# Exchanging the engines of two products in a selective-scan kernel: VectorE multiplies by B, GpSimd by C, in one ring of nine tiles

## The chip, the cores and the metric

The kernel runs on one core of a Trainium2 chip. The metric is the device time of one execution in microseconds; the figure for a kernel is the median of its runs. Before the change that is 13688.56 us (three runs, 13686.65 to 13699.43).

Engine names in the profile: PE is TensorE (PEld its weight loads), DVE is VectorE, ACT is ScalarE, POOL is GpSimd, SP is SyncE, whose queue issues all DMAs of this kernel.

## The reference, cut to what matters

The program is four network layers in a row on a 4 x 64 x 64 x 128 input. Layers 0 and 1 hold selective scans over images of L = 4096 pixels; layers 2 and 3 (a gated neighbourhood layer and a window attention) are not touched. The scan, for every image, direction k (4), channel d and state n (16), is

```
dA = exp(delta_t[d] * A[d, n])
h  = dA * h + (delta_t[d] * u_t[d]) * B_t[n]
y_t[d] = sum over n of h[d, n] * C_t[n]
```

Layer 0 has 128 channels, layer 1 has 256; B and C depend on time and state, not on the channel. Softplus, normalisation, 3x3 convolutions and projections stand before and after.

## The kernel before, in words

**Tiling.** A *unit* is a group of 8 channels x 16 states, which fills 128 partitions, by TS = 1024 pixels in fp32. 16 units (NG) make a *step*: 128 channels, one direction, a quarter of the image. 16 steps make a *task* (NU = 256 units): one image and 128 channels. There are 4 tasks in layer 0 and 8 in layer 1, so 12 x 256 = 3072 units, 1536 pairs and 192 steps.

**What a unit does.** `load` (L436) has the SP queue fetch delta*u of the 8 channels from DRAM, each repeated over the 16 states, into a tile `dub`. `times_b` (L443) multiplies it on GpSimd by `repB`, B repeated over the channels in SBUF by a DMA (`repeat`, L371), and writes one half of a two-unit tile `h`. `decay` has TensorE spread delta over the states into a PSUM tile `da` (L451, two buffers) and ScalarE turn it into exp(delta*A) in place (L453). `scan` (L462) is VectorE's recurrence, in place on `h`. After each second unit VectorE multiplies the pair by C (L472), from `h` into another tile `hc`; C is a PSUM tile of one buffer that `bring_c` (L492) makes with TensorE once a step. `save` (L483) has ScalarE copy the last column of the states for the next step. `add_up` (L547) has TensorE sum `hc` over the states into a PSUM tile `yps`, which `sum_so_far` opens and `keep` (L557) copies out.

**The order.** No scheduler moves these instructions: `run` writes the order out by hand, one pass of its loop per unit u, and each engine takes its own instructions in that order. In pass u: scan(u); times_b(u+3); bring_c at the first unit of a step; save of the pair just ended; decay(u+2); add_up of the pair just ended; then pieces of the *preparation* of a later step (`prepare`: delta, delta*u and their DMAs `dud`, `dp`, `repB`), begun AHEAD = 22 units early, and pieces of *side work* (convolutions, projections and norms before and after the scans, helpers at L97); then load(u+6). A small model of each engine's backlog, `Plan`, decides how many pieces fit into a pass: `slot` enters what the pass itself costs TensorE, ScalarE and GpSimd, and a piece is taken if the engines would reach it soon enough. DMAs of a step are posted with due times in units (`post`). When all scans are done, a rest of layer 1 runs, then layers 2 and 3.

**Buffers.** `dub` has 5 tiles of one unit, `h` 3 tiles of two units, `hc` 2 tiles of two units, `da` 2 and `C` 1 (PSUM), `repB` and `dp` 2.

Of the kernel before, what the change touches and what calls it, by code (L numbers as in the profile page):

```python
# [9 lines left out]
F32 = mybir.dt.float32  # L10
# [7 lines left out]
P = 128  # L18
H = 64
# [5 lines left out]
NS = 16  # L25
ND = 4
NG = 16
TS = 1024
# [77 lines left out]
UNIT = 3.6  # L106
# [7 lines left out]
class Plan:  # L114
# [22 lines left out]
    def post(self, chain, issue, due=0.0):  # L137

        if self.running:
            self.posted.append((chain, max(self.done, due), issue))  # L140
        else:
            issue()
# [11 lines left out]
    def slot(self, u, sums, copies):  # L154
        at = self.at
        self.now = u * UNIT
        self.flush()
        at["PE"] = max(at["PE"], self.now) + 1.1
        at["ACT"] = max(at["ACT"], at["PE"]) + 1.1
        at["POOL"] = max(at["POOL"], self.now - 1.2) + 2.4  # L160
        at["PE"] += sums
        at["ACT"] += copies

# [56 lines left out]
class ScanWeights:  # L220


    def __init__(self, tc, C, pool, layer, d_xp, d_dtw, d_av):
        nc = tc.nc
        self.layer, self.nct, self.rank = layer, TILES[layer], RANKS[layer]
        nct, rank = self.nct, self.rank
        self.nc, self.pool, self.d_xp, self.d_dtw = nc, pool, d_xp, d_dtw
        n = ND * nct * NG
        av = pool.tile([P, n + 2 * ND * nct], F32, name=f"av{layer}")
        nc.sync.dma_start(out=av, in_=d_av)  # L230
        self.a = av[:, 0:n]
        nc.scalar.activation(self.a, self.a, AF.Exp)
        nc.vector.tensor_scalar_mul(self.a, self.a, -1.0)
        self.dtb = av[:, n : n + ND * nct].rearrange("p (k t) -> p k t", k=ND)
        ds = av[:, n + ND * nct :].rearrange("p (t k) -> p t k", t=nct)
        self.dsum = pool.tile([P, nct], F32, name=f"dsum{layer}")
        nc.vector.reduce_sum(self.dsum, ds, axis=AX.X)

        self.pick = pool.tile([P, P], F32, name=f"pick{layer}")
        one, two = (C.ident[:, i * H + rank + NS : i * H + rank + 2 * NS] for i in range(2))  # L240
        both = [P, NS, P // NS]
        nc.vector.tensor_add(
            self.pick.rearrange("p (n i) -> p n i", n=NS),
            one.unsqueeze(2).to_broadcast(both),
            two.unsqueeze(2).to_broadcast(both),
        )
# [24 lines left out]


NU = ND * NSTEP * NG
AHEAD = 22


class Scans:
# [47 lines left out]
    def prepare(self, t, step):  # L325

        nc, W, half, post = self.plan, t.W, self.half, self.plan.post
        begin = self.plan.now
        k, c = t.steps[step]
        R = W.rank  # L330
# [35 lines left out]
        out = t.prepared[step] = {"xd": xd}  # L366

        def repeat():
            out["B"] = self.tile("repB", 2)
            src = bass.AP(xdd.tensor, xdd.offset + R * TS, [[TS, NS], [0, 8], [1, TS]])  # L370
            nc.sync.dma_start(out=out["B"], in_=src)  # L371

        post("rep", repeat, max(begin + 5 * UNIT, ready))

        bias = W.dtb[:, k, t.ct : t.ct + 1]
        delta, low = self.tile("delta", 1), self.tile("low", 1)
        for i in range(HALVES):
# [5 lines left out]
                start=True,  # L383
# [25 lines left out]
        def own(part, j):  # L409
            if j == part == 0:  # L410
                out["delta"] = self.tile("dp", 2, shape=(96, 4, TS), dtype=BF16)
            nc.sync.dma_start(
                out=out["delta"][32 * part : 32 * part + 32, j, :], in_=parts[32 * j : 32 * j + 32, part, :]
            )

        for i in range(12):
            j, part = divmod(i, 3)
            post("rep", lambda part=part, j=j: own(part, j), begin + (9 + 0.7 * i) * UNIT)
        yield ""

    def unit(self, u):
# [7 lines left out]
    def load(self, u):  # L429
        t, step, jj, j, g = self.unit(u)  # L430
        if g == 0:
            self.plan.flush("prep")
        dud = t.prepared[step]["du"]
        dub = self.live["dub", u] = self.tile("dub", 5)
        src = bass.AP(dud.tensor, dud.offset + 8 * g * TS, [[0, NS], [TS, 8], [1, TS]])
        self.nc.sync.dma_start(out=dub, in_=src)  # L436

    def times_b(self, u):
        t, step, jj, j, g = self.unit(u)
        if u % 2 == 0:  # L440
            self.live["h", u // 2] = self.tile("h", 3, shape=(P, 2, TS))
        dbu = self.live["h", u // 2][:, u % 2, :]
        self.nc.gpsimd.tensor_mul(dbu, self.live.pop(("dub", u)), t.prepared[step]["B"])  # L443

    def decay(self, u):
        t, step, jj, j, g = self.unit(u)
# [8 lines left out]
    def scan(self, u):  # L455

        nc = self.nc
        t, step, jj, j, g = self.unit(u)
        way = slice(None, None, -1) if t.steps[step][0] >= 2 else slice(None)
        da, pair = self.live.pop(("da", u)), self.live["h", u // 2]  # L460
        h = pair[:, u % 2, :]
        nc.vector.tensor_tensor_scan(  # L462
            h[:, way],
            da[:, way],
            h[:, way],
            0.0 if step % NSTEP == 0 else t.states[step - 1][:, u % NG : u % NG + 1],
            ALU.mult,
            ALU.add,
        )
        if u % 2:  # L470
            hc = self.live["hc", u // 2] = self.tile("hc", 2, shape=(P, 2, TS))
            nc.vector.tensor_mul(hc, pair, t.prepared[step]["C"].unsqueeze(1).to_broadcast([P, 2, TS]))  # L472

    def save(self, p):

        t, step, jj, j, g = self.unit(2 * p)
        pair = self.live.pop(("h", p))
        i = 2 * p % NG
        if i == 0:
            t.states[step] = self.tile("state", 2, shape=(P, NG))  # L480
        if step % NSTEP < NSTEP - 1:
            end = 0 if t.steps[step][0] >= 2 else TS - 1
            self.nc.scalar.copy(t.states[step][:, i : i + 2], pair[:, :, end])  # L483

    def bring_c(self, u):

        t, step, jj, j, g = self.unit(u)
        c = t.prepared[step]["C"] = self.psum.tile([P, TS], F32, name="C", tag="C", bufs=1)
        rows = t.W.rank + 2 * NS
        for i in range(HALVES):  # L490
            at = slice(i * H, i * H + rows)
            self.nc.tensor.matmul(  # L492
                c[:, self.half(i)], t.W.pick[at, :], t.prepared[step]["xd"][at, :], start=True, stop=True
            )


# [36 lines left out]

    def add_up(self, p):

        hc = self.live.pop(("hc", p))
        for v in range(2):
            t, step, jj, j, g = self.unit(2 * p + v)
            for i in range(HALVES):
                at = i * H + 32 * v  # L540
                out = self.live["yps"][at : at + 32, :]
                if t.steps[step][0] % 2 == 0:
                    rhs = hc[:, v, self.half(i)]
                else:
                    rhs = hc[:, v, :].rearrange("p (r i l) -> p r i l", i=HALVES, l=ROWS)[:, :, i, :]
                    out = out.rearrange("p (r l) -> p r l", l=ROWS)
                self.nc.tensor.matmul(out, self.C.gather[jj], rhs, start=False, stop=jj == 3)  # L547
# [19 lines left out]
    def run(self, between):  # L567
# [7 lines left out]
            pass  # L575
        self.plan.start()
        pieces, fetch, fetched = Lane(self.plan, "prep", iter(())), iter(()), 0
        for u in range(-7, total):
            if u >= 0:
                self.scan(u)  # L580
            if 0 <= u + 3 < total:
                self.times_b(u + 3)
            if u >= 0 and u % NG == 0:
                self.bring_c(u)
            if u > 0 and u % 2 == 0:
                self.save(u // 2 - 1)
            if 0 <= u + 2 < total:
                self.decay(u + 2)
            if u > 0 and u % 2 == 0:
                self.add_up(u // 2 - 1)  # L590
            if u > 0 and u % 8 == 0:
                self.keep(u - 1)
            if u > 0 and u % 8 == 1:
                self.sum_so_far(u - 1)
            even, eighth, first_one = u % 2 == 0, u % 8 == 1, u % NG == 0
            self.plan.slot(
                u, 1.6 * even + 1.0 * eighth + 2.0 * first_one, 0.25 * even + 0.7 * (u % 8 == 0)
            )
            ahead, rest = divmod(u + AHEAD, NG)
            if rest == 0:  # L600
# [19 lines left out]
            if u >= 0:  # L620
# [1 line left out]
                if self.later:  # L622
                    self.later.pop(0)()
                between(n, i)
            if 0 <= u + 6 < total:
                self.load(u + 6)
        self.add_up(total // 2 - 1)
        self.save(total // 2 - 1)
        self.keep(total - 1)
        while self.later:  # L630
            self.later.pop(0)()

# [524 lines left out]
def scan_layers(tc, C, nb, x_in, d0, s0, d1, s1, out):  # L1157

    nc = tc.nc
    with ExitStack() as es:  # L1160
# [24 lines left out]
        def between(n, i):  # L1185
# [1 line left out]
            nonlocal lane, current, credit  # L1187
            u = n * NU + i

            done = group[n] - (1 if i >= 8 or n and group[n - 1] == group[n] else 2)  # L1190
            left, rate = -(lane.count if lane else 0), 0.0
            for name, b, after, before in ([current] if lane else []) + work:
                left += PIECES[name]
# [15 lines left out]
        with tc.manual_schedule():  # L1209
            for _ in side.pre0(0):  # L1210
# [8 lines left out]
                Aside(side, n, spans, bank)  # L1219
                for n, bank in enumerate(  # L1220
                    lambda name=name, bufs=bufs: psum.tile([P, TS], F32, name=name, tag=name, bufs=bufs)[:, 0:T]
                    for name, bufs in (("C", 1), ("da", 2))
                )
            ]
            lanes = [lane.post1(nb - 1, range(n, NCH, 3), wt) for n, lane in enumerate(lanes)]
# [959 lines left out]
```

## Time and profile before

| what | value |
|---|---|
| median of three runs | 13688.56 us |
| the profiled execution, own time | 13702.12 us |
| its span (first to last instruction) | 13699.8 us |
| first scan starts, last product with C ends | 204.7 us, 11445.5 us |
| VectorE, GpSimd busy over the span | 11766.7 us (86%), 9928.8 us (72%) |
| TensorE, ScalarE busy over the span | 10024.2 us (73%), 7913.4 us (58%) |
| mean granted TensorE clock | 0.737 of full |
| DMA: bytes, share of 16 engines' span | 2474.92 MB, 73.6% (the SP queue) |

How to read it: the profile records each instruction's engine, line, start and length. A line of the groups gives line, engine and operation, what is written and read, the count, then total busy time and mean ns of one, then the engine's idle time just before such instructions and what ended it. A line of the waits says which engine, at which line, was let go by what, with total us, how often, and the longest. The timeline gives start, length and instruction in order of time, neighbours of one kind merged. L97 is the helper through which all preparation and side work passes.

### The profile page before, as it was taken

The page shows a single profiled execution, that of the slowest core. Times are in us where ns is not written, and L with a number is a line of the kernel's source. Part 1 is how long each engine was busy: PE and PEld are TensorE (multiplying, and loading weights), DVE is VectorE, ACT ScalarE, POOL GpSimd, SP SyncE. Part 2 cuts the span into 40 slices and gives each one's busy share as a digit, 9 for nine tenths or more (in the row PEclk, how much of TensorE's full clock was granted, in tenths as well). Part 3 has the DMA queues.
Part 4 walks back from the last instruction along what each step waited for, and adds up shares of the span by engine and source line. Part 5 has one row for each costly group of instructions (what it writes and reads, how often), then busy time and mean ns, then how long its engine had stood idle before and what let it go on. Part 6 is the DMA issues. An engine that isn't in the chain of part 4 may idle for free. (4 is left out here: it accounts for less than half of the span.)

```text
span 13699.8 us, 121257 instructions
## 1 busy us (share of the span) xinstructions
PE 10024.2 (73%) x37178; PEld 2510.6 (18%) x37178; DVE 11766.7 (86%) x6980; ACT 7913.4 (58%) x10594; POOL 9928.8 (72%) x4754
## 2 busy tenths in 40 slices
PE   5777777777777777767777677777777776666688
PEld 1111111111111111111111111111111111111455
DVE  3998899989999899989999899999999994577555
ACT  3666566655665466645665555555555554665577
POOL 3787788878887788868887888888888884355200
PEclk7666767776777776667777777777777776888899
DMA  5888888898888888888889888878888784234300
GB/s 153 204 213 217 208 207 219 214 216 201 204 219 207 193 216 202 211 212 199 196 215 220 210 197 199 203 192 202 202 197 201 193 194 107 70 97 107 73 20 17
DMA packets 877057, 2474.92 MB, mean 181 GB/s; under 512 B 142455, under 2 KB 164095, under 8 KB 868215
## 3 DMA queue, kind: packets, MB, share of 16 engines
q1 hardware_dynamic: 876407, 2467.18, 73.6%
q8 instruction: 295, 4.83, 0.2%
q14 instruction: 355, 2.91, 0.1%
HBM read 2043.34 MB, written 272.37 MB: 169 GB/s over the span
## 5 line engine op out<-in xcount | busy, mean ns | idle before, releaser
L443 POOL TENSOR_TENSOR h<-dub,repB 128x1024 f32<-128x1024 f32 x3072 | 7176.1, 2357 | 1307.6 <-DMA dub<-dud 945.6
L462 DVE TENSOR_TENSOR_SCAN h<-da,state,h 128x1024 f32<-128x1024 f32 x2304 | 5324.5, 2340 | 493.6 <-POOL h L443 225.2
L453 ACT ACTIVATE da<-da,av 128x1024 f32<-128x1024 f32 x3072 | 3339.6, 1088 | 2955.6 <-PE da L451 2937.7
L451 PE MATMUL da<-dp,spread 96*128 96x512 bf16 x6144 | 2521.9, 504 | 2285.6 <-DVE h L462 2221.2
L472 DVE TENSOR_TENSOR hc<-h,C 128x2048 f32<-128x2048 f32 x1536 | 3513.6, 2288 | 115.9 <-PE C L492 42.9
L547 PE MATMUL yps<-hc,gather 128*32 128x512 f32 x12288 | 2444.3, 880 | 5.6 <-DVE hc L472 5.6
L462 DVE TENSOR_TENSOR_SCAN h<-da,h 128x1024 f32<-128x1024 f32 x768 | 1731.6, 2280 | 353.4 <-POOL h L443 250.3
L451 PEld LDWEIGHTS <-spread 96*128 96x128 bf16 x6144 | 550.1, 107 | 5618.7 <-issue 5484.7
L97 POOL TENSOR_TENSOR delta<-delta,low 128x1024 f32<-128x1024 f32 x192 | 451.5, 2352 | 553.2 <-ACT low L97 499.0
L97 PE MATMUL ms<-d,wts 128*128 128x512 f32 (+3 forms) x900 | 674.2, 876 | 229.7 <-POOL d L97 137.2
L97 ACT ACT_TABLE_LOAD x600 | 769.8, 1283 | 16.2 <-PE ms L97 5.4
L97 PE MATMUL ms<-xd,xpdt 8*128 8x512 f32 (+1 forms) x768 | 626.9, 907 | 134.3 <-ACT xd L97 33.8
L97 ACT CAST parts<-delta 128x1024 bf16<-128x1024 f32 x384 | 400.7, 1043 | 435.3 <-POOL delta L97 409.4
L1896 POOL COPY wide_total<-total 128x128 f32<-128x128 f32 x128 | 37.6, 293 | 828.1 <-DVE total L1894 641.7
L97 ACT ACTIVATE low<-ms,av 128x512 f32<-128x512 f32 x384 | 264.0, 687 | 528.2 <-PE ms L97 507.5
L530 PE MATMUL yps<-y,ident 128*128 128x512 f32 x576 | 508.2, 972 | 78.9 <-ACT y L557 78.7
L97 POOL TENSOR_TENSOR low<-delta,xc 128x1024 f32<-128x1024 f32 x192 | 502.6, 2617 | 2.7
L1452 ACT ACTIVATE hid<-hid,relb 128x1024 f32<-128x1024 f32 x288 | 323.0, 1146 | 264.6 <-DVE hid L1447 264.4
L1865 ACT ACTIVATE s<-s,least 128x512 f32<-128x512 f32 x512 | 372.4, 727 | 178.6 <-DVE least L1852 177.4
L1852 DVE CUSTOM_DVE_ANT_0 s<-sps,bias 128x512 f32<-128x512 f32 x512 | 323.5, 687 | 175.6 <-PE sps L1841 164.6
L1554 POOL TENSOR_TENSOR acc<-acc,part 128x1024 f32<-128x1024 f32 x120 | 313.3, 2617 | 214.1 <-DVE part L1548 186.9
L547 PEld LDWEIGHTS yps<-hc,gather 128*32 128x32 f32 x12288 | 282.4, 127 | 1007.8 <-issue 999.6
(284 smaller groups left out, 11119.9 us busy)
## 6 DMA issues: line engine op xcount, KB each, us to landing
dub<-dud SPq DMA_DIRECT2D x3072, 512.0 KB
dp<-parts SPq DMA_DIRECT2D x2304, 64.0 KB
repB<-xdd SPq DMA_DIRECT2D x192, 512.0 KB
dud<-low SPq DMA_DIRECT2D x192, 512.0 KB
spread<-gd SPq DMA_DIRECT2D x72, 1024.0 KB
pad<-xid SPq DMA_DIRECT2D x192, 256.0 KB
szd<-o SPq DMA_DIRECT2D x96, 256.0 KB
xcd<-o SPq DMA_DIRECT2D x96, 256.0 KB
```

The source lines that it names most:

```text
L97: return call(*args, **kw)
L443: self.nc.gpsimd.tensor_mul(dbu, self.live.pop(("dub", u)), t.prepared[step]["B"])
L451: self.nc.tensor.matmul(da[:, cols], self.C.spread[:, jj, :], dp[:, j, cols], start=True, stop=True)
L453: self.nc.scalar.activation(da, da, AF.Exp, scale=t.W.a[:, at : at + 1])
L462: nc.vector.tensor_tensor_scan(h[:, way], da[:, way], h[:, way], 0.0 if step % NSTEP == 0 else t.states[step - 1][:, u % NG : u % NG + 1], ...
L472: nc.vector.tensor_mul(hc, pair, t.prepared[step]["C"].unsqueeze(1).to_broadcast([P, 2, TS]))
L530: self.nc.tensor.matmul(self.like_part(yps, k), self.C.ident, self.part(t.y, k, c, b), start=True, stop=False)
L547: self.nc.tensor.matmul(out, self.C.gather[jj], rhs, start=False, stop=jj == 3)
L1452: nc.scalar.activation(hid, hid, AF.Gelu, bias=self.relb[:, m, t : t + 1])
L1554: (nc.vector if alone and pair else nc.gpsimd).tensor_add(acc, acc, part)
L1852: self.nc.vector.tensor_tensor_reduce(out=self.live["s", n][:, h, :], in0=self.live["sps", n][:, h, :], in1=self.bias[case][:, h, :], scal ...
L1865: self.nc.scalar.activation(s, s, AF.Exp, scale=-1.0, bias=self.live["least", n][:, h : h + 1], accum_out=self.live["total", n][:, h : h + 1],
```

## The change

VectorE and GpSimd exchange their products. The unit's DMA writes delta*u straight into a half of `h`; VectorE multiplies both halves by B in place, one pass before the first of the two is scanned; the scans run in place; GpSimd multiplies both halves by C in place; TensorE sums `h` itself. `dub` and `hc` are gone and `h` has nine tiles of two units. B is now the PSUM tile made by TensorE, two passes before its step, behind the decay of the step's first unit; C is the tile repeated in SBUF by a DMA. The loads run LEAD = 10 units ahead of the scan, and add_up, keep and sum_so_far run LAG = 4 units behind it. The preparation of a step begins 28 units early. The plan enters GpSimd's work as 4.5 us per pair. The program's reserved DMA scratch memory is made smaller.

```diff
 # Plan.slot
-        at["POOL"] = max(at["POOL"], self.now - 1.2) + 2.4
+        if u % 2 == 0:
+            at["POOL"] = max(at["POOL"], self.now) + 4.5
...
-AHEAD = 22
+AHEAD = 28
+LEAD = 10
+LAG = 4
...
 # Scans.prepare
-            out["B"] = self.tile("repB", 2)
-            src = bass.AP(xdd.tensor, xdd.offset + R * TS, [[TS, NS], [0, 8], [1, TS]])
-            nc.sync.dma_start(out=out["B"], in_=src)
-        post("rep", repeat, max(begin + 5 * UNIT, ready))
+            out["C"] = self.tile("repC", 2)
+            src = bass.AP(xdd.tensor, xdd.offset + (R + NS) * TS, [[TS, NS], [0, 8], [1, TS]])
+            nc.sync.dma_start(out=out["C"], in_=src)
+        post("rep", repeat, max(begin + 15 * UNIT, ready))
...
-            post("rep", lambda part=part, j=j: own(part, j), begin + (9 + 0.7 * i) * UNIT)
+            post("rep", lambda part=part, j=j: own(part, j), begin + (11 + 0.5 * i) * UNIT)
...
 # Scans.load
-        dub = self.live["dub", u] = self.tile("dub", 5)
+        if u % 2 == 0:
+            self.live["h", u // 2] = self.tile("h", 9, shape=(P, 2, TS))
-        self.nc.sync.dma_start(out=dub, in_=src)
-    def times_b(self, u):
-        t, step, jj, j, g = self.unit(u)
-        if u % 2 == 0:
-            self.live["h", u // 2] = self.tile("h", 3, shape=(P, 2, TS))
-        dbu = self.live["h", u // 2][:, u % 2, :]
-        self.nc.gpsimd.tensor_mul(dbu, self.live.pop(("dub", u)), t.prepared[step]["B"])
+        self.nc.sync.dma_start(out=self.live["h", u // 2][:, u % 2, :], in_=src)
+    def times(self, engine, p, name):
+        t, step, jj, j, g = self.unit(2 * p)
+        pair = self.live["h", p]
+        engine.tensor_mul(pair, pair, t.prepared[step][name].unsqueeze(1).to_broadcast([P, 2, TS]))
...
 # Scans.scan
-        if u % 2:
-            hc = self.live["hc", u // 2] = self.tile("hc", 2, shape=(P, 2, TS))
-            nc.vector.tensor_mul(hc, pair, t.prepared[step]["C"].unsqueeze(1).to_broadcast([P, 2, TS]))
...
 # Scans.run
-        for u in range(-7, total):
-            if u >= 0:
+        for u in range(-12, total + LAG + 1):
+            v = u - LAG
+            if 0 <= u < total:
                 self.scan(u)
-            if 0 <= u + 3 < total:
-                self.times_b(u + 3)
-            if u >= 0 and u % NG == 0:
-                self.bring_c(u)
-            if u > 0 and u % 2 == 0:
+            if u % 2 and -1 <= u < total - 1:
+                self.times(self.nc.vector, (u + 1) // 2, "B")
+            if 0 < u <= total and u % 2 == 0:
                 self.save(u // 2 - 1)
+                self.times(self.nc.gpsimd, u // 2 - 1, "C")
             if 0 <= u + 2 < total:
                 self.decay(u + 2)
-            if u > 0 and u % 2 == 0:
-                self.add_up(u // 2 - 1)
+                if (u + 2) % NG == 0:
+                    self.bring_b(u + 2)
+            if v > 0 and v % 2 == 0:
+                self.add_up(v // 2 - 1)
...
-            if 0 <= u + 6 < total:
-                self.load(u + 6)
+            if 0 <= u + LEAD < total:
+                self.load(u + LEAD)
...
-    nc = bacc.Bacc("TRN2", target_bir_lowering=False, num_devices=1)
+    nc = bacc.Bacc("TRN2", target_bir_lowering=False, num_devices=1, dynamic_dma_scratch_size=1024)
```

`keep` and `sum_so_far` take v in place of u in the same way, and `bring_b` is `bring_c` with the columns of B (`pick` selects them).

More of the change, by code (lines that the diff above doesn't have):

```diff
@@ L239, in __init__ @@
         self.pick = pool.tile([P, P], F32, name=f"pick{layer}")
-        one, two = (C.ident[:, i * H + rank + NS : i * H + rank + 2 * NS] for i in range(2))
+        one, two = (C.ident[:, i * H + rank : i * H + rank + NS] for i in range(2))
         both = [P, NS, P // NS]
@@ L469, in scan @@
         )
-        if u % 2:
-            hc = self.live["hc", u // 2] = self.tile("hc", 2, shape=(P, 2, TS))
-            nc.vector.tensor_mul(hc, pair, t.prepared[step]["C"].unsqueeze(1).to_broadcast([P, 2, TS]))
     def save(self, p):
         t, step, jj, j, g = self.unit(2 * p)
-        pair = self.live.pop(("h", p))
+        pair = self.live["h", p]
         i = 2 * p % NG
@@ L483, in save, with bring_b @@
             self.nc.scalar.copy(t.states[step][:, i : i + 2], pair[:, :, end])
-    def bring_c(self, u):
+    def bring_b(self, u):
         t, step, jj, j, g = self.unit(u)
-        c = t.prepared[step]["C"] = self.psum.tile([P, TS], F32, name="C", tag="C", bufs=1)
+        rep = t.prepared[step]["B"] = self.psum.tile([P, TS], F32, name="B", tag="B", bufs=1)
         rows = t.W.rank + 2 * NS
@@ L492, in bring_c @@
             self.nc.tensor.matmul(
-                c[:, self.half(i)], t.W.pick[at, :], t.prepared[step]["xd"][at, :], start=True, stop=True
+                rep[:, self.half(i)], t.W.pick[at, :], t.prepared[step]["xd"][at, :], start=True, stop=True
             )
@@ L534, in add_up @@
     def add_up(self, p):
-        hc = self.live.pop(("hc", p))
+        hc = self.live.pop(("h", p))
         for v in range(2):
@@ L577, in run @@
         pieces, fetch, fetched = Lane(self.plan, "prep", iter(())), iter(()), 0
-        for u in range(-7, total):
-            if u >= 0:
+        for u in range(-12, total + LAG + 1):
+            v = u - LAG
+            if 0 <= u < total:
                 self.scan(u)
-            if 0 <= u + 3 < total:
-                self.times_b(u + 3)
-            if u >= 0 and u % NG == 0:
-                self.bring_c(u)
-            if u > 0 and u % 2 == 0:
+            if u % 2 and -1 <= u < total - 1:
+                self.times(self.nc.vector, (u + 1) // 2, "B")
+            if 0 < u <= total and u % 2 == 0:
                 self.save(u // 2 - 1)
+                self.times(self.nc.gpsimd, u // 2 - 1, "C")
             if 0 <= u + 2 < total:
                 self.decay(u + 2)
-            if u > 0 and u % 2 == 0:
-                self.add_up(u // 2 - 1)
[L591 to L595, printed above, removed]
+                if (u + 2) % NG == 0:
+                    self.bring_b(u + 2)
+            if v > 0 and v % 2 == 0:
+                self.add_up(v // 2 - 1)
+            if v > 0 and v % 8 == 0:
+                self.keep(v - 1)
+            if 0 < v < total and v % 8 == 1:
+                self.sum_so_far(v - 1)
+            if u >= total:
+                continue
+            even, first_one = u % 2 == 0, u % NG == NG - 2
             self.plan.slot(
-                u, 1.6 * even + 1.0 * eighth + 2.0 * first_one, 0.25 * even + 0.7 * (u % 8 == 0)
+                u, 1.6 * even + 1.0 * (v % 8 == 1) + 2.0 * first_one, 0.25 * even + 0.7 * (v % 8 == 0)
             )
@@ L624, in run @@
                 between(n, i)
-            if 0 <= u + 6 < total:
-                self.load(u + 6)
-        self.add_up(total // 2 - 1)
-        self.save(total // 2 - 1)
-        self.keep(total - 1)
+            if 0 <= u + LEAD < total:
+                self.load(u + LEAD)
         while self.later:
@@ L1188, in between @@
             u = n * NU + i
-            done = group[n] - (1 if i >= 8 or n and group[n - 1] == group[n] else 2)
+            done = group[n] - (1 if i >= 8 + LAG or n and group[n - 1] == group[n] else 2)
             left, rate = -(lane.count if lane else 0), 0.0
@@ L1221, in scan_layers @@
                     lambda name=name, bufs=bufs: psum.tile([P, TS], F32, name=name, tag=name, bufs=bufs)[:, 0:T]
-                    for name, bufs in (("C", 1), ("da", 2))
+                    for name, bufs in (("B", 1), ("da", 2))
                 )
```

## The prediction

> **What bounds the kernel now.** I first cut the span at the first scan (204.7 us) and at the end of the last product with C (11446 us), since the change touches only what lies between. In the windows the columns are: stretch and its us, then busy us of TensorE, its weight loads, VectorE, ScalarE and GpSimd, the granted clock, the DMA share and GB/s.
>
> ```profile
> 204.70:4000.00 3795.30, 2866.55 (x9072) 568.51 (x9071) 3491.58 (x1541) 2281.68 (x2771) 3068.26 (x1419) 0.69 0.86 211
> 4000.00:8000.00 4000.00, 2945.50 (x9641) 594.24 (x9638) 3656.08 (x1613) 2302.75 (x2829) 3215.95 (x1489) 0.71 0.86 208
> 8000.00:11000.00 3000.00, 2187.75 (x6706) 496.99 (x6705) 2883.47 (x1277) 1665.70 (x2132) 2617.12 (x1197) 0.74 0.81 198
> ```
>
> VectorE is busy 92%, 91% and 96%: it is the bound of the scan stage, GpSimd is next (81%, 80%, 87%). Then VectorE's timeline in a quiet place, to see what it does at its best:
>
> ```profile
> 8413.55 2.29 DVE L472 TENSOR_TENSOR hc<-h,C 128x2048 f32<-128x2048 f32 x1
> 8415.75 4.59 DVE L462 TENSOR_TENSOR_SCAN h<-da,state,h 128x1024 f32<-128x1024 f32 x2
> 8420.38 2.29 DVE L472 TENSOR_TENSOR hc<-h,C 128x2048 f32<-128x2048 f32 x1
> ```
>
> A pair of units, two scans and one product, takes 8420.38 - 8413.55 = 6.83 us with no gap. 1536 pairs make 10,490 us; the stage takes 11,241 us. So at most some 750 us can be won in it, and the waits of VectorE within it say where they are:
>
> ```profile
> DVE h L462 <- ACT da L453: 300.9, 310, 13.4
> DVE h L462 <- POOL h L443: 290.1, 145, 14.1
> DVE h L462 <- ACT state L483: 57.3, 66, 6.3
> DVE hc L472 <- PE C L492: 42.9, 36, 4.2
> ```
>
> About 290 us are waits for GpSimd's product with B. Why GpSimd is late, though it is busy only 80 to 87%, its own waits tell:
>
> ```profile
> POOL h L443 <- DMA dub<-dud: 934.6, 372, 17.8
> POOL delta L97 <- ACT low L97: 463.0, 112, 11.9
> ```
>
> and the SP queue, whose loads stand still until GpSimd has freed one of the five `dub` tiles:
>
> ```profile
> SPq L436 <- POOL h L443: 3494.1, 1607, 13.7
> ```
>
> So the loop load, GpSimd, scan has too little lead for what a load needs when other transfers lie before it. Pairing the nth load with the nth product, the 371 products that waited for a load began a median of 8.6 us and at most 21.3 us after its issue; a load was planned only three passes (3 x 3.41 = 10 us) ahead of its product.
>
> **VectorE's own work.** One product of 2048 elements from SBUF and PSUM per pair goes (L472, 2288 ns) and one of the same shape and places comes (h times B). Cost 0, the pair stays at 6.83 us. The product used to depend on the scan just before it; now the scan depends on the product just before it; one such dependence each. The scan then carries two waits where the old product carried one; a scan let go by GpSimd in the trace starts 0.04 us after its end, as the old product did after its scan. 0 to 0.05 us x 1536 = 0 to 77 us; I take 0, since those rows are the nearest.
>
> **The wait for GpSimd's product with B.** It goes: -290 us. In its place VectorE waits for the load itself. The load of unit w is issued in pass w-10 and used in pass w-1 or w-2, so 8 passes = 27 us of lead against 8.6 (21 at most) us needed. Its tile must be free: the ring of nine pairs gives the slot back when TensorE's sum of the pair 18 units before is done, which stands in pass w-12, two passes ahead of the load. What can eat the lead is the SP queue: the twelve `dp` loads of a step are posted behind `repC`, which is not due until 15 units, so they now go out in one bunch instead of between the unit loads. In a busy place of the trace `dp` loads leave some 1.9 us apart (the queue waits for older transfers), so a bunch can hold the unit loads up for 12 x 1.9 = 23 us; with 8.6 us to land that is 4 us over the lead in the worst steps. With perhaps one step in eight like that I take 24 x 1 us, say 25 us; bounds 0 and the old 290. The DMA work itself is unchanged in bytes and about 2% denser in time: the stage's 0.81 to 0.86 share becomes 0.83 to 0.88.
>
> **GpSimd.** 3072 products of 1024 become 1536 of 2048. No row shows the new form. By the rows of 1024 (2357 ns, L443) a pair costs 2 x 2357 = 4714 ns. The row d<-d,big of 512 elements takes 1269 ns, so an element is (2357 - 1269) / 512 = 2.125 ns and the fixed part 181 ns: a pair should cost 4533 ns. In place is free (delta<-delta,low, 2352 ns). The far end is strided reading: low<-delta,xc takes up to 2942 ns, twice that is 5880; but the new operands are contiguous rows, so I take 4.53. [...]
>
> Is there room? A step of 16 units takes VectorE 8 x 6.83 = 54.6 us. GpSimd needs 8 x 4.53 = 36.2, the four preparation products 2.35 + 2.62 + 2.13 + 2.13 = 9.2, side work some 420 / 192 = 2.2: 47.6 us, 87%. Adding what it lost waiting for ScalarE's `low` (514 / 192 = 2.7 us) it is 92%. The wait added: the product with C waits for the scan and, as it overwrites `h`, for ScalarE's save, which stands behind one exp. From the scan's end that is 0.05 + 1.0 + 1.1 + 0.2 = 2.4 us (the TensorE, exp and copy lengths in the timeline), then 4.5 us of work: done 6.9 us after the scan. TensorE asks for it four passes later, behind decay(u+6): 18.3 us + 1 us. So 12 us of slack. Queued behind that wait on TensorE are the decays, and behind them exp and the scan; behind the product on GpSimd the preparation products, and ScalarE's casts after them. I take 25 us for the times when 12 us are not enough; 0 and 300 are the bounds.
>
> **B in PSUM.** `bring_b` stands in pass u = 14 of a step behind decay(u+2), which must wait for the end of scan(u); B is wanted when scan(u+1) ends, 2.3 us later. In the profile:
>
> ```profile
> 9011.83 0.38 PE L451 MATMUL da<-dp,spread 96*128 96x512 bf16 x1
> 9012.14 1.13 PE L492 MATMUL C<-xd,pick 40*128 40x512 f32 x4
> ...
> 2750.11 2.08 PE L492 MATMUL C<-xd,pick 36*128 36x512 f32 x4
> ```
>
> The four matmuls take 1.13 us at a high clock, 2.08 at a low one, after 0.8 to 1.0 us for the decay: B is there after 1.9 to 3.1 us. VectorE waits 0 to 0.8 us a step; 192 x 0.3 = 58 us, in place of C's 43: +15 us.
>
> **The waits for da** (301 + 57 us) come from TensorE and ScalarE pieces in front of a decay. The window from one scan to the next but one is the same, 4.5 us, so I leave them. Some of the pieces were late because GpSimd was; I take -25 us (0 to -150). More lead for `dp` and a pass shift elsewhere: 0, hidden under the scans. The end: GpSimd's 4.5 us replaces VectorE's 2.3 before the last sum: +2 us. Layers 2 and 3 (2254 us after the stage) stay.
>
> Sum: -290 + 25 + 25 + 15 - 25 + 2 = -248 us. On the profiled execution's 13702: 13,454; the median of the runs lies 13.6 us lower, so 13,440.
>
> **Rivals.**
> *GpSimd becomes the bound (slower).* Place: product with C, TensorE's sum, the decays queued behind it. Its step becomes longer than VectorE's 54.6 us when a pair costs over (54.6 - 11.4) / 8 = 5.4 us (5.1 with the `low` waits), and longer than the present 11241 / 192 = 58.5 us when it costs over 5.9 (5.55). At the strided row's 5.88 the step is 58.4 us, plus about 2 us of `low` waits: 192 x 60.4 = 11,600, +360 us: 14,050. For it: the new form is in no row, and in-order waits at 92% load may queue. Against: contiguous rows all lie at 2.13 to 2.36 us per 1024. [...]
> *The wait returns as another.* DVE waits for loads behind the `dp` bunch, or for da behind a blocked sum: some 170 us more than I took, 13,610.
> *The da waits shrink too.* If half of the 358 us hung on GpSimd's lateness, another -150 us: 13,290.
> *It doesn't do what it says:* the built order of both programs shows 1536 products with B on VectorE one pass ahead and 1536 with C on GpSimd; ruled out.
>
> **How the numbers follow.** Forecast 13,440 (13,340 to 13,540) 0.55; shrinking da waits 0.12; the wait returns 0.14, of which 0.06 end within 0.2% (27 us, about what a measurement of this kernel tells from no change); GpSimd bound, or its queue, 0.19. So faster 0.75, same 0.06, slower 0.19. The range 13,290 to 13,800 leaves out half of the gain's rival and some two thirds of the slower one.
>
> **What would show it.** VectorE's waits: no GpSimd row, a small DMA row, B near 58 us, da near 330. GpSimd's new row at 4.5 us. TensorE's waits: L547 for GpSimd under 100 us. GpSimd's row over 5.1 us, or L547 waiting for hundreds of us, would make it wrong; so would a DMA row at VectorE's product of over 150 us.

## The result, and the profile after

The changed kernel takes 13747.0 us (median of five runs, 13740.3 to 13752.1), the kernel before beside it 13697.22 us (five runs): ratio 1.0038, 95% interval 1.0023 to 1.0052. It is slower by some 50 us, where I forecast 248 us less. The profiled execution of after has an own time of 13747.0 us, a span of 13745.1 us and a mean granted clock of 0.744 (before 0.737). The scan stage, from the start of the first scan to the end of the last, went from 11238.5 to 11276.6 us: +38 us of the 45 us between the two profiled executions.

In the same three windows as before, GpSimd is no busier (2968, 3172 and 2532 us; before 3068, 3216 and 2617) and VectorE is busy 91%, 92% and 95% (92%, 91% and 96%). GpSimd did not become the bound: its new product takes 4530 ns, and TensorE's sum waited for it once in the stage.

```profile
L446 POOL TENSOR_TENSOR h<-h,repC 128x2048 f32<-128x2048 f32 x1536 | 6951.4, 4530 | 1708.5 <-ACT state L483 1370.7 <-DVE h L465 211.9 <-issue 44.6
...
PE yps L547 <- POOL h L446: 3.2, 1, 3.2
```

VectorE's waits in the stage show what changed (engine, line, what let it go, us in total, times, longest):

```profile
DVE h L465 <- ACT da L456: 524.7, 428, 10.4
DVE h L446 <- issue: 70.4, 59, 7.9
DVE h L446 <- PE B L492: 68.7, 32, 13.4
...
DVE h L446 <- DMA h<-dud: 6.7, 5, 3.0
```

The 290 us for GpSimd are gone. The waits for da, 300.9 + 57.3 us before, are 524.7. At the product with B stand waits for B and waits that the profile can put down to nothing ("issue"). The groups of VectorE give the idle time in full (line, engine, operation, names, shape, count, then busy us and mean ns, then idle us and what ended it), of before and of after:

```profile
L462 DVE TENSOR_TENSOR_SCAN h<-da,state,h 128x1024 f32<-128x1024 f32 x2304 | 5324.5, 2340 | 493.6 <-POOL h L443 225.2 <-ACT da L453 219.4 <-ACT state L483 41.4
L472 DVE TENSOR_TENSOR hc<-h,C 128x2048 f32<-128x2048 f32 x1536 | 3513.6, 2288 | 115.9 <-PE C L492 42.9 <-remote 10.7 <-DVE h L462 0.5
L462 DVE TENSOR_TENSOR_SCAN h<-da,h 128x1024 f32<-128x1024 f32 x767 | 1729.3, 2280 | 168.0 <-ACT da L453 81.4 <-POOL h L443 64.8 <-ACT state L483 15.9
...
L465 DVE TENSOR_TENSOR_SCAN h<-da,state,h 128x1024 f32<-128x1024 f32 x2304 | 5319.1, 2340 | 519.9 <-ACT da L456 401.5 <-DVE h L446 4.1 <-ACT d L97 0.9
L446 DVE TENSOR_TENSOR h<-h,B 128x2048 f32<-128x2048 f32 x1536 | 3476.9, 2264 | 363.7 <-DMA h<-dud 190.4 <-issue 70.4 <-PE B L492 68.7
L465 DVE TENSOR_TENSOR_SCAN h<-da,h 128x1024 f32<-128x1024 f32 x768 | 1727.6, 2281 | 160.8 <-ACT da L456 123.2 <-DVE h L446 1.4 <-ACT state L483 0.5
```

Of after's 363.7 us before the product, 183.7 lie before the very first one (it starts the stage), so 180 us are waits within it, 173.5 of them before the first product of a step, where B is new (before: 69.7). Cleared in the same way, VectorE's idle time in the stage was 493.6 + 168.0 us at the scans and 115.9 at the product before; it is 519.9 + 160.8 and 180.0 now: 777.5 against 860.7, +83 us. Its busy time in these three groups fell by 46 us, from 10569.7 to 10523.6 (mostly the product, 2264 ns in place of 2288). +83 - 46 = +37, which is the stage's +38. So a gain of 290 was paid back in full on the same engine.

Where the idle time hides outside the waits, the timeline of VectorE in a quiet place shows:

```profile
8421.70 4.59 DVE L465 TENSOR_TENSOR_SCAN h<-da,state,h 128x1024 f32<-128x1024 f32 x2
8426.21 2.26 DVE L446 TENSOR_TENSOR h<-h,B 128x2048 f32<-128x2048 f32 x1
8428.57 4.62 DVE L465 TENSOR_TENSOR_SCAN h<-da,state,h 128x1024 f32<-128x1024 f32 x2
8433.11 2.26 DVE L446 TENSOR_TENSOR h<-h,B 128x2048 f32<-128x2048 f32 x1
```

The product of 8426.21 ends at 8428.47, and the scan that reads its result starts at 8428.57, 0.10 us later. The next product works on another pair: it starts at 8433.11, 0.08 us before the scan's recorded end (8433.19). The pair takes 6.90 us here against 6.83 in the lines shown of before; over all undisturbed pairs the medians are 6.874 against 6.825 us with a state and 6.754 against 6.705 without.

### The profile page after: what moved, and what is told of

Same layout as the page of the kernel before. It is cut to its first block, busy times and chain, and to the rows that moved or that the text cites. A ratio compares the mean times of both kernels' runs of the same rounds, so it can differ in the third digit from the quotient of the medians.

```text
span 13745.1 us, 120368 instructions
## 1 busy us (share of the span) xinstructions
PE 9945.1 (72%) x37178; PEld 2503.4 (18%) x37178; DVE 11718.9 (85%) x6980; ACT 7914.9 (58%) x10594; POOL 9719.0 (71%) x3218
## 5 line engine op out<-in xcount | busy, mean ns | idle before, releaser
L446 POOL TENSOR_TENSOR h<-h,repC 128x2048 f32<-128x2048 f32 x1536 | 6951.4, 4530 | 1708.5 <-ACT state L483 1370.7
L465 DVE TENSOR_TENSOR_SCAN h<-da,state,h 128x1024 f32<-128x1024 f32 x2304 | 5319.1, 2340 | 519.9 <-ACT da L456 401.5
L454 PE MATMUL da<-dp,spread 96*128 96x512 bf16 x6144 | 2481.8, 496 | 2302.3 <-DVE h L465 2275.6
L446 DVE TENSOR_TENSOR h<-h,B 128x2048 f32<-128x2048 f32 x1536 | 3476.9, 2264 | 363.7 <-DMA h<-dud 190.4
L547 PE MATMUL yps<-h,gather 128*32 128x512 f32 x12288 | 2424.3, 874 | 3.2 <-POOL h L446 3.2
L465 DVE TENSOR_TENSOR_SCAN h<-da,h 128x1024 f32<-128x1024 f32 x768 | 1727.6, 2281 | 160.8 <-ACT da L456 123.2
L97 PE MATMUL ms<-xd,xpdt 8*128 8x512 f32 (+1 forms) x768 | 599.2, 870 | 220.7 <-ACT delta L97 71.9
L547 PEld LDWEIGHTS yps<-h,gather 128*32 128x32 f32 x12288 | 281.7, 127 | 1089.4 <-issue 846.3
L97 PE MATMUL ms<-pad,diag 96*32 96x504 f32 (+1 forms) x2304 | 398.9, 801 | 108.8 <-DMA pad<-xid 80.5
```

The lines of the kernel that those rows point to most:

```text
L97: return call(*args, **kw)
L446: engine.tensor_mul(pair, pair, t.prepared[step][name].unsqueeze(1).to_broadcast([P, 2, TS]))
L454: self.nc.tensor.matmul(da[:, cols], self.C.spread[:, jj, :], dp[:, j, cols], start=True, stop=True)
L465: nc.vector.tensor_tensor_scan(h[:, way], da[:, way], h[:, way], 0.0 if step % NSTEP == 0 else t.states[step - 1][:, u % NG : u % NG + 1], ...
```

## The experiments

My theory after this result: the wait for GpSimd went as planned, and three costs took its place: the product right in front of the scan that needs it, B made too late, and more waiting for da. For the last I first held the bunch of `dp` loads behind `repC` responsible. The rivals: the bound of the stage is not VectorE's waits at all, so that what is taken away at one place comes back at the next; or GpSimd's slack behind the scans is short. In the expectations theory 1 is the account that I held at that point and theory 2 its rival. Ratios are to the kernel before, measured again beside them (medians 13692.28 to 13695.31 us), with the 95% interval.

### e1_spread_dp: the dp loads no longer behind repC

After, with `repC` in a chain of its own and the `dp` loads spread.

```diff
-        post("rep", repeat, max(begin + 15 * UNIT, ready))
+        post("repc", repeat, max(begin + 15 * UNIT, ready))
-            post("rep", lambda part=part, j=j: own(part, j), begin + (11 + 0.5 * i) * UNIT)
+            post("rep", lambda part=part, j=j: own(part, j), begin + (11 + 0.9 * i) * UNIT)
```

> The changed kernel, but the twelve dp loads of a step are no longer held behind repC: repC has a chain of its own and the dp loads fall due 0.9 units apart. Theory 1 (the bunch of dp loads on the SP queue delays pad and xd loads behind it, TensorE waits for these in order, and the decays behind them come late): VectorE's waits for da fall from 525 us to about 420, TensorE's waits for pad and xd from 108 us to under 40, time 13,747 - 100 = about 13,650. Theory 2 (TensorE and ScalarE are simply the second bound, and any wait removed returns as a wait for da): within 30 us of 13,747.

Measured: 13737.73 us, 1.0032 (1.0021 to 1.0044). The waits for da went from 524.7 to 497.1 us, and the product's idle time rose from 180 to 202. TensorE's waits for the loads `pad` and `xd` fell from 108.5 us only to 77.4, not under 40. Theory 2's range held: the bunch behind `repC` was worth some 9 us, and it is not what makes da late. Whether `pad` and `xd` loads that come late for another reason do, this run does not settle.

### e2_early_b: B ahead of the decay

After, with `bring_b(u + 2)` placed before `decay(u + 2)`, so that TensorE makes B before it waits for the end of scan(u).

```diff
-                self.decay(u + 2)
                 if (u + 2) % NG == 0:
                     self.bring_b(u + 2)
+                self.decay(u + 2)
```

> The changed kernel with bring_b ahead of decay(u+2) instead of behind it. Theory 1: VectorE's waits for B fall from 69 us to under 20 and da does not change, so -40 to -60 us, about 13,700. Theory 2: no change, 13,720 to 13,770.

Measured: 13671.86 us, 0.9985 (0.9977 to 0.9992), 75 us under after. The group of the product:

```profile
L446 DVE TENSOR_TENSOR h<-h,B 128x2048 f32<-128x2048 f32 x1535 | 3471.5, 2262 | 87.7 <-PE B L492 50.0 <-issue 14.2 <-POOL pad L97 6.7
```

Its idle time fell from 180 to 88 us, and the waits for da stayed (529.0). So about half of the time that B cost was its place. The named waits for B fell to 50.0 us, not under 20. How late it came in after, the timeline shows where scan(u) has just ended (at 9240.4):

```profile
9238.18 4.47 DVE L465 TENSOR_TENSOR_SCAN h<-da,h 128x1024 f32<-128x1024 f32 x2
...
9240.52 1.01 PE L454 MATMUL da<-dp,spread 96*128 96x512 bf16 x2 [1.09 <-DVE h L465]
...
9241.47 2.08 PE L492 MATMUL B<-xd,pick 40*128 40x512 f32 x4
...
9243.65 2.29 DVE L446 TENSOR_TENSOR h<-h,B 128x2048 f32<-128x2048 f32 x1 [1.00 <-PE B L492]
```

The decay can start only at the end of scan(u) and takes 1.01 us, the four matmuls of B take 2.08 us, and the product starts 1.00 us late. Whether the four matmuls take 2.08 or 1.13 us goes with the clock that TensorE was granted. The windows of after just before and around this place give busy us of TensorE, its weight loads, VectorE, ScalarE and GpSimd, then the granted clock, DMA share and GB/s:

```profile
9229.70:9233.12 3.42, 0.00 (x0) 0.00 (x0) 2.45 (x2) 2.81 (x5) 3.42 (x2) 1.00 0.18 73
9233.12:9253.60 20.48, 16.66 (x43) 3.67 (x43) 19.17 (x10) 7.19 (x9) 20.48 (x7) 0.50 0.73 176
```

The clock is 0.50 while B is made; in the prediction's two lines of before it was 1.00 (1.13 us) and 0.50 (2.08 us). Counted over the steps after the first, after made B at 0.50 in 98, at full clock in 76 and across a change in 17; e2 in 79, 102 and 10. The median of one matmul therefore jumps from one length to the other on a small shift. The rows of L492 of after, of e2 and of e3 (duration of one in ns: min/median/max):

```profile
L492 PE MATMUL B<-xd,pick x768: 589/1054/1220, 194.2 to 11425.4; 40*128 40x512 f32 x128, 36*128 36x512 f32 x64
L492 PE MATMUL B<-xd,pick x768: 589/693/1220, 193.2 to 11335.6; 40*128 40x512 f32 x128, 36*128 36x512 f32 x64
L492 PE MATMUL B<-xd,pick x768: 589/1031/1221, 195.2 to 11208.7; 40*128 40x512 f32 x128, 36*128 36x512 f32 x64
```

The lengths reach from 0.59 to 1.22 us in all three. B stands ahead of the decay in e2 and in e3, and the median is 693 ns in one and 1031 in the other; C at its old place has 714 ns in before and 1054 in e4. So the place does not set the length. What e2 wins is that B no longer waits for the end of scan(u). Of what it has left, 55 us lie in 13 waits of over 2 us.

### e3_mid_product: the product between two scans that do not need it

e2, with VectorE's product with B one scan earlier: after the first scan of a pair, for the next pair. B is made one pass earlier.

```diff
-            if u % 2 and -1 <= u < total - 1:
-                self.times(self.nc.vector, (u + 1) // 2, "B")
+            if u % 2 == 0 and -2 <= u < total - 2:
+                self.times(self.nc.vector, u // 2 + 1, "B")
+            if 0 <= u + 3 < total and (u + 3) % NG == 0:
+                self.bring_b(u + 3)
```

> The changed kernel with VectorE's product with B one scan earlier, between the two scans of the pair before it, and bring_b one pass earlier. No scan then follows the product that it depends on. Theory 1 (the gap of 0.10 us between the product and the scan that depends on it is a term of its own, where independent instructions overlap by 0.08 us): pair period 6.87 to 6.69 us, 1536 x 0.19 = -290 us, less what returns as waits: about 13,500. Theory 2: da waits swallow most of it, over 13,650.

Measured: 13528.32 us, 0.9880 (0.9865 to 0.9895), 144 us under e2. VectorE in a quiet place:

```profile
9007.76 2.26 DVE L446 TENSOR_TENSOR h<-h,B 128x2048 f32<-128x2048 f32 x1
9009.94 4.58 DVE L465 TENSOR_TENSOR_SCAN h<-da,state,h 128x1024 f32<-128x1024 f32 x2
9014.44 2.26 DVE L446 TENSOR_TENSOR h<-h,B 128x2048 f32<-128x2048 f32 x1
```

```profile
DVE h L465 <- ACT da L456: 637.1, 399, 14.1
```

Now every instruction starts before the recorded end of the one ahead of it, and a pair takes 6.68 us in place of 6.87. That alone would be 0.19 x 1536 = 292 us. About half came back: the waits for da rose from 529.0 to 637.1 us and the product's idle time from 87.7 to 126.1, together 146 us, which leaves 146; 144 were measured.

### e4_deep_dub: the kernel before, with more lead for its loads

Before, with eight `dub` tiles in place of five, loads nine units ahead in place of six, the preparation three units earlier. The DMAs of the preparation stay due in the same passes, and the reserved DMA scratch memory is that of after. No product changes its engine. This takes away the wait for GpSimd by its cause.

```diff
-AHEAD = 22
+AHEAD = 25
...
-        dub = self.live["dub", u] = self.tile("dub", 5)
+        dub = self.live["dub", u] = self.tile("dub", 8)
...
-            if 0 <= u + 6 < total:
-                self.load(u + 6)
+            if 0 <= u + 9 < total:
+                self.load(u + 9)
```

> The kernel before, both products where they were, with eight dub tiles in place of five, the load of a unit nine passes ahead in place of six, the preparation begun three units earlier and its DMAs due in the same passes as before. It takes away the late loads alone. Theory 1: VectorE's waits for GpSimd fall from 290 us to under 80 and its waits for da stay near 360, so about 13,697 - 220 = 13,480. Theory 2: da waits grow by most of what is won, 13,600 to 13,700.

Measured: 13530.15 us, 0.9880 (0.9867 to 0.9894), 163 us under before. Its waits:

```profile
DVE h L462 <- ACT da L453: 402.5, 323, 12.8
DVE h L462 <- ACT state L483: 66.9, 57, 8.1
...
DVE h L462 <- POOL h L443: 26.7, 33, 5.7
```

The wait for GpSimd fell from 290.1 to 26.7 us, -263, and the waits for da rose from 358 to 469, +111. So removing the wait was worth some 160 us, not 290, with everything else in place. Counted by step, the scans' waits for ScalarE rose by 88 us in the 59 of 192 steps in which VectorE's other waits fell by more than 1 us, and by 17 in all the others: da is late where VectorE no longer stops for GpSimd. The two readings that I held both missed: the gain is neither whole nor lost.

### e5_late_c: e4, with the product with C one scan later

The same move as e3 on the other kernel: VectorE's product with C stands after the first scan of the next pair (`h` with 4 tiles, `dub` 7, loads eight ahead; C, the sums and their copies a pass or two later).

```diff
-        if u % 2:
-            hc = self.live["hc", u // 2] = self.tile("hc", 2, shape=(P, 2, TS))
-            nc.vector.tensor_mul(hc, pair, t.prepared[step]["C"].unsqueeze(1).to_broadcast([P, 2, TS]))
...
+            if 0 < u <= total and u % 2 == 0:
+                self.save(u // 2 - 1)
+                self.times_c(u // 2 - 1)
```

> The deep_dub kernel (both products where they were before) with VectorE's product with C one scan later, between the two scans of the next pair, C brought one pass later and add_up two passes behind; h has four tiles, dub seven with loads eight passes ahead. No product then follows the scan that it depends on. Theory 1 (the gap between dependent neighbours on VectorE is a term of its own whatever the operands): pair period 6.83 to 6.70 us, 1536 x 0.12 = -180 us, of which half returns as waits for da because the window for a decay shrinks by 0.12 us: about 13,530 - 90 = 13,440. Theory 2 (the gap belonged to the in-place product with B): period stays 6.83, 13,530 or slower.

Measured: 13445.68 us, 0.9823 (0.9808 to 0.9839): under both kernels, by some 250 us and 300 us, with the engines left as they were.

```profile
8416.55 2.26 DVE L475 TENSOR_TENSOR hc<-h,C 128x2048 f32<-128x2048 f32 x1
8418.73 4.58 DVE L462 TENSOR_TENSOR_SCAN h<-da,state,h 128x1024 f32<-128x1024 f32 x2
8423.23 2.26 DVE L475 TENSOR_TENSOR hc<-h,C 128x2048 f32<-128x2048 f32 x1
```

The pair is at 6.68 us here too; the product that depended on the scan just before it had also cost something. Median pairs went from 6.825 to 6.682 us. Of 0.143 x 1536 = 220 us, 85 us arrived at the end (13530.15 - 13445.68); the wait for GpSimd came back in part, with VectorE faster and with one `dub` tile and one pass of lead less than in e4:

```profile
DVE h L462 <- ACT da L453: 470.0, 372, 13.6
...
DVE h L462 <- POOL h L443: 131.0, 92, 6.7
```

### e6_unit34: e3, with the plan's pass at 3.4 us

```diff
-UNIT = 3.6
+UNIT = 3.4
```

> The mid_product kernel with the plan's UNIT at 3.4 us in place of 3.6. Theory 1 (waits for da grow as VectorE gets faster because the plan still counts on 3.6 us a pass and puts too many pieces before a decay): waits for da fall from 637 us to under 500, 13,528 - 120 = about 13,410. Theory 2 (the waits for da come from the work that TensorE and ScalarE have to do between the scans, wherever it is put): within 40 us of 13,528.

Measured: 13514.63 us, 0.9872 (0.9856 to 0.9889), 14 us under e3; the waits for da 620 us against 637. Theory 2's range held: the plan's pace is not what makes da late.

### e7_lead11 and e8_lead8: longer and shorter lead of the loads

e7 is e3 with loads 11 units ahead, e8 is e2 with 8 (10 in both before).

```diff
-LEAD = 10
+LEAD = 11
```

> The mid_product kernel with LEAD at 11 in place of 10, so that the load keeps the lead that it had before the product moved a scan earlier. Theory 1 (loads are not what VectorE waits for): -20 to -50 us, the 57 us that its product waits for loads, da unchanged, 13,490. Theory 2 (the ring's slots come free too late, the SP queue stands and everything behind it is late): slower than 13,528.

> The early_b kernel with LEAD at 8 in place of 10, the ring unchanged. The slot that a load needs is then free four passes before the load instead of two, so the SP queue stands less on the ring and comes earlier to the pad and xd loads behind. Theory 1 (the part of the da waits that the change has over deep_dub, 529 to 470 us, comes from loads for side work that stand behind unit loads on the SP queue): da waits near 470, 13,672 - 60 = about 13,610. Theory 2 (it comes from elsewhere; a shorter lead only lets loads land late): 13,660 to 13,720, with the product with B waiting more for its load.

Measured: e7 13542.83 us, 0.9891 (0.9876 to 0.9906), 15 us over e3, which its interval does not tell from e3; e8 13699.31 us, 1.0003 (0.9995 to 1.0011), 27 us over e2. In e7 the product's named waits for its load fell from 30.3 to 7.5 us, and those for da rose from 637 to 671. In e8 it is the other way round:

```profile
DVE h L465 <- ACT da L456: 471.2, 402, 9.1
DVE h L446 <- DMA h<-dud: 73.1, 24, 10.1
```

da falls from 529 to 471 as theory 1 said, but the load, which was almost never late in after, is now late, and the time is theory 2's. The queue's own wait, for TensorE's sum to free a slot of the ring, was 2652.2 us in after. Within one window of the stage (208 to 11200 us) it is 708.8 us in e8 against 2434.9 in e2, and 3401.9 in e7 against 2209.6 in e3. So a load that is issued before its slot is free does hold the SP queue up.

That this is what makes da late does not follow. Counted by step, 56 us of e8's fall in the waits for da lie in the 20 steps in which the product's own waits rose by more than 1 us (by 94 us together), and 3 us in all the others. A new wait covered da, as the wait for GpSimd had covered it before. Of e7's rise, 21 of 34 us lie in the 9 steps in which the product's waits fell. And in e4, with fewer waits for da than after (402.5 us), the queue stands longer for its slots (after, then e4):

```profile
SPq L440 <- PE yps L547: 2652.2, 633, 11.5
SPq L436 <- POOL h L443: 3372.6, 1498, 15.0
```

### e9_lag2: e2, with the sums two passes behind in place of four

```diff
-LAG = 4
+LAG = 2
```

> The early_b kernel with LAG at 2 in place of 4: TensorE sums a pair two passes earlier, so the ring's slot is free two passes earlier and the SP queue stands less, but TensorE asks for GpSimd's product with C after about 5 us of slack instead of 12. Theory 1 (SP queue): da waits fall by some 60 us unless TensorE waits for GpSimd, 13,610 to 13,670. Theory 2 (the slack of 12 us is what keeps GpSimd off the path): L547 waits for GpSimd by more than 100 us, da grows, over 13,720.

Measured: 13727.1 us, 1.0024 (1.0013 to 1.0034), 55 us over e2. TensorE's sum now waits for GpSimd, and the scans behind it for da:

```profile
PE yps L547 <- POOL h L446: 283.6, 327, 2.7
```

```profile
DVE h L465 <- ACT da L456: 654.7, 532, 15.3
```

In after the first of these is 3.2 us. Two passes are too few and four are enough. The queue stood only 673.2 us for slots here (same window as above), yet da is later than in e2: behind TensorE's new wait this run cannot show what a freer queue is worth.

## Why the prediction was wrong

**What held.** GpSimd's new row is 4530 ns, against 4533 worked out; TensorE's sum waits 3.2 us for it, so the term "GpSimd +25" was about 0. VectorE waits for loads 6.7 us, so "loads +25" was too high. The wait for GpSimd, 290 us, is gone. The main slower rival, GpSimd as the bound, did not happen. (Of the 514 us that I put down to `low`, 463.0 were waits for it and 51.0 for ScalarE's save; GpSimd's 92% stays.)

**Step 1 that failed: "Cost 0, the pair stays at 6.83 us".** I had given 0 to 77 us and took 0. Median pairs are 0.049 us longer: 0.049 x 1536 = 75 us, the far end. Over all gaps the medians are: an instruction that depends on nothing just before it starts 0.083 to 0.085 us before the recorded end of its neighbour; the old product, which needed the scan just before it, 0.034 us after it; the new scan, which needs the product just before it and da as well, 0.104 us after it. The product itself gives back 0.024 us. I had drawn the price from a scan let go by GpSimd, the nearest row by the waiting instruction but not by the engine that releases it. Where a scan waits for da in any case, this gap is inside the wait, so that 75 is an upper figure. That the order is the cause is shown: e3 and e5 move this product, with what feeds it, and the pair falls to 6.68 us in both kernels. Two waits alone do not cost it: in before every scan waits for GpSimd's product and for da and still starts 0.083 us early. Beside a dependence on the neighbour, which of the two differences makes 0.104 out of 0.034, the second wait or the producer, no run separates. By these runs the product's place was worth 0.14 us a pair (6.825 to 6.682 us, e5) to 0.19 us (6.87 to 6.68 us, e3).

**Step 2: "VectorE waits 0 to 0.8 us a step; 192 x 0.3 = 58 us".** The term of B measured 180 us, 0.94 us a step. The mechanism was right and its size was off, in two ways. In the 98 steps with B made at half clock the wait was 1.20 us in the mean (median 0.94), where I had 0.8 for the worst. And 18 steps waited over 2 us, 76 us together, for which the term had nothing: in all but one of them the product starts 0.10 us after B's last matmul, so TensorE had come to B late. What makes the clock fall no run shows. In the stretch shown under e2 TensorE did nothing from 9229.70 to 9233.12 us, and the clock was 0.50 behind it. That is not the usual case: of the 628 falls of the clock in after's stage, 22 had TensorE under 2% busy in the 3.41 us before, and in the median it was 38% busy.

**Step 3: "The window from one scan to the next but one is the same, 4.5 us, so I leave them ... I take -25 us".** This is the largest miss: 358 us became 525, +167. The window did stay (4.48 to 4.50 us in before, 4.53 to 4.55 in after); the "so" failed. First, e4 takes away the wait for GpSimd and leaves the products, and the waits for da rise by 111 us, nearly all of it in the steps where the other wait fell: while VectorE stood waiting for GpSimd, da had time to come, and without that stop its lateness is seen. A wait that is removed uncovers what it covered. So even its pure gain was 163 us. Second, da is 55 us higher in after than in e4, and the cause of that stays open. I had the loads that stand in the SP queue for a free slot in mind; e7, e8 and e4 do not bear it out.

**The sum.** Forecast and result lie 298 us apart. The waits for da make 192 of it (+167 in place of -25), the first products of the steps 89 (+104 in place of +15), the pair up to 75; loads and GpSimd were 40 us cheaper than the 50 taken. That is 316, with 75 as an upper figure.

**The exchange itself.** e3 and e4, with opposite engines, are at 13,528 and 13,530 us, but that is a coincidence of sums: e3 has its product between scans that do not need it, e4 has not. Like with like, the exchanged kernel is the slower: by 142 us where the product depends on its neighbour or feeds it (e2 over e4), by 83 us where it does not (e3 over e5). So the gain that I forecast did not need the exchange: more lead for the loads (e4) and the product's place (e5) won 247 us without it.

**Still open.** e3 has 637 us of waits for da where e5 has 486 (470.0 + 16.3 for the state) and 131 for GpSimd. With the products' own idle time (126.1 us against 37.6) the sums are 763 and 655, and the medians of these two kernels with the same pair time lie 83 us apart. What makes da later in e3 is not settled; the window from one scan to the next but one is 4.34 to 4.36 us in both, so it is not that. A third `da` buffer was not tried. The mean granted clock also differs between profiled executions (0.737 in before, 0.752 in e4, 0.750 in e2, 0.742 in e5), and before alone has the larger DMA scratch memory; no run separates either.

## What to carry to other kernels

Before a wait on the bounding engine is counted as a gain, ask which other feeds of the same engine it covers: here 111 of 263 us came back as the next late feed. On the engine that bounds (VectorE, 91% to 95% busy in after's three windows) put something independent between a producer and its consumer; here that was worth 0.14 to 0.19 us for each pair of about 6.8 us, of which a third to a half reached the end. Something that is made once a step belongs ahead of the per-unit wait on its engine, not behind it (75 us here), and matmuls in a kernel whose clock changes should be priced at both lengths (1.13 and 2.08 us for the four of a step here). When an experiment adds one wait and another shrinks, look whether both happen in the same steps before the second is called a gain.

## What the runs showed of the hardware that I had not expected

Among VectorE's scans and products in the stage, the median start of an instruction relative to the recorded end of its neighbour was -0.083 us when independent (before and after), +0.034 when the product with C needed the scan (before), and +0.104 when the scan needed the product with B and waited for ScalarE's da as well (after). The same matmul of 512 columns in fp32, making B, took 0.59 to 0.69 us at the full granted clock and about 1.06 or 1.22 at 0.50 in after. In after's trace the granted clock knew only these two values and kept each for multiples of 3.41 us (all but one of 1396 stretches); the mean of 0.74 is a mix of the two. VectorE's product in place with B (2264 ns) was 24 ns shorter than the one into another tile with C (2288 ns), but e5's product into another tile also took 2260, so what goes with the shorter time is that it no longer depends on the scan just before it.
